# A state space block whose rows of B are spread from DRAM, with the first group's work divided differently

## The chip, the cores and the metric

The kernel runs on one core of a Trainium2 chip. Its time is the device time of one execution in microseconds (us); where several executions were timed, the median is given. The core's engines work side by side and each runs its own instructions in order: TensorE (PE in the profile, its weight loads PEld), VectorE (DVE), ScalarE (ACT), GpSimd (POOL), and SyncE (SP), which issues nearly all DMA transfers.

## The reference

The input is 16 sequences of 256 tokens with 128 features, in float32. Four blocks follow one another, each added to its input after a layer norm: a state space block, a local attention block with a feed-forward part (two layers), a power attention block, and the local attention block again. The change touches the first one, cut here to its core:

```python
x = resid * rsqrt(mean(resid**2) + 1e-5) * norm_w
skip, xe = x @ skip_w.T, x @ in_w.T
xs = silu(causal_conv4(xe) + conv_b)              # 256 channels
delta = softplus(xs @ wd1.T @ wd2.T + wd2_b)
A = -exp(A_log); Bm = xs @ wb.T; Cm = xs @ wc.T   # 16 states
h[t] = exp(delta[t] * A) * h[t-1] + (delta[t] * xs[t]) * Bm[t]
y[t] = sum over states of h[t] * Cm[t]
out = resid + ((y + xs * W_D) * silu(skip)) @ out_w.T
```

## The kernel before, in words

**Tiles.** The state space block (`ssm_block`) takes two sequences at a time as a group: 8 groups of 512 columns (C), the 256 channels as two halves of 128 partitions (e = 0 and 1). The 16 states of a group are 16 ticks, 128 ticks in all. A tick is: `spread` (a DMA that copies one row of B to all 128 partitions, tile bb, 256 KB, four buffers), `decay` (two ScalarE exponentials into PSUM, tile a, two of them in turn), `inputs` (GpSimd, bx = dx * bb, 128x1024), `scan` (VectorE, hs), `rows_of_c` (TensorE spreads a row of C into PSUM, c_ps, one bank), `products` (hs * c on VectorE, or on GpSimd for ticks 0, 3 and 8) and `add` (TensorE adds to y_ps).

**A group's preparation.** `moments_of` (VectorE) and `factors` (GpSimd) give the norm's scales; `normed_rows` (ScalarE) writes four tiles of rows, xr; `turn` (TensorE) transposes them into xrT_ps and `turned` (ScalarE) reads that into xrT; `conv` multiplies by the four taps' weights cw, eight products of 512 columns for the two halves, into xe_ps; `conv_out` (ScalarE) reads it into xs. `rows` and `reps` multiply xs by the weights of delta and C, and of B. For B the weights are repeated eight times (wrep, lines 152 to 162), so that `reps` gives a 128-row tile in which row p is B's row p mod 16; `reps_out` copies it to SBUF, and `spread` reads its eight equal rows, each for 16 partitions (line 354). `steps_in`, `steps_out` and `logs` give the two terms of softplus, and `steps` (GpSimd) adds them, giving delta, and multiplies by xs, giving dx, for each half.

**Order.** Each engine's instructions are pinned to the order in which the program issues them (class `Pinned`). The first group's preparation is written out by hand (lines 427 to 510): the weights cw are made (the weights transposed into in_w_ps, multiplied by the taps on VectorE, transposed into cw_ps half by half, each half copied to SBUF by ScalarE), then normed rows, turn, convolution, and so on through `steps`, the first two decays, the casts `second` and `third`, the first two `inputs` (lines 503 and 504), and then the normed rows, the turn and half of the convolution of the second group. Everything after that follows a written list (`written`, line 521), one round per group: each word is a step with its tick and its lag in groups. In it the read of a group's convolution (`co0`) stands ahead of the decays of ticks 2 and on, a group's `ro` (reps_out) stands between the spreads of ticks 12 and 13 of the group before (`sp12`, `sp13`), and its own first spread (`sp0`) follows three ticks later. After scan 0 and each third scan, one step of `fill` is run: a load or a preparation for the later blocks' weights (line 557), among them the scales of q and k (qs), which GpSimd multiplies into the rotation tables (rope).

Of the kernel before, what the change touches and what calls it, by code (L numbers as in the profile page):

```python
# [12 lines left out]
F32 = mybir.dt.float32  # L13
# [7 lines left out]
P = 128  # L21
D = 128
L = 256
E = 256
NST = 16
# [20 lines left out]
def kernel(ctx: ExitStack, tc: tile.TileContext, io, out: bass.AP):  # L46
    nc = tc.nc
# [13 lines left out]
    ident = const.tile([P, P], F32, name="ident")  # L61
# [5 lines left out]
    ones = const.tile([P, L], F32, name="ones")  # L67
# [51 lines left out]
    def ssm_block(fill):  # L119
        es = ExitStack()  # L120
        w = es.enter_context(tc.tile_pool(name="ssm_w", bufs=1))
        prep = es.enter_context(tc.tile_pool(name="ssm_prep", bufs=1))
        work = es.enter_context(tc.tile_pool(name="ssm_work", bufs=4))
        ps_m = es.enter_context(tc.tile_pool(name="ssm_psm", bufs=1, space=PSUM))
        ps_a = es.enter_context(tc.tile_pool(name="ssm_psa", bufs=1, space=PSUM))
        ps_c = es.enter_context(tc.tile_pool(name="ssm_psc", bufs=1, space=PSUM))
# [7 lines left out]
        NE = E // P  # L134
# [11 lines left out]
        def quarters(t):  # L146
            return t.rearrange("p (j i n) -> p j i n", j=NQ, i=2)

        wall = w.tile([P, NE, P], F32, name="wall")

        NR = P // NST
        wrep = w.tile([P, NE, P], F32, name="wrep")
        for e in range(NE):
            part = slice(e * P, (e + 1) * P)
            nc.sync.dma_start(quarters(wall[:, e])[:, :, 0, :], io["wd1T"][part].rearrange("p (j n) -> p j n", j=NQ))
            nc.sync.dma_start(
                quarters(wall[:, e])[:, :, 1, :], io["wcT"][part].unsqueeze(1).to_broadcast([P, NQ, NST])
            )
            nc.sync.dma_start(
                wrep[:, e].rearrange("p (j n) -> p j n", j=NR),  # L160
                io["wbT"][part].unsqueeze(1).to_broadcast([P, NR, NST]),
            )
        wd2T = w.tile([P, E], F32, name="wd2T")
        nc.gpsimd.memset(wd2T, 0.0)
        for j in range(NQ):
# [8 lines left out]
        pe, dve, act, pool, sp = (Pinned(e) for e in (nc.tensor, nc.vector, nc.scalar, nc.gpsimd, nc.sync))  # L174
# [4 lines left out]
        C = GS * L  # L179
# [3 lines left out]
        def bank(shape, name):  # L183
            return ps_m.tile(shape, F32, name=name, tag="m")
# [4 lines left out]
        for i in range(2):  # L189
            t = ps_a.tile([P, NE, GS, L], F32, name=f"a{i}")  # L190
# [4 lines left out]
        for i in range(2):  # L195
            t = w.tile([P, GS, PAD + L], F32, name=f"xrT{i}")
# [3 lines left out]
        groups = [{} for _ in range(NG)]  # L200
# [27 lines left out]
        def scaled(q, h, a, tag):  # L228
            t = prep.tile([P, GT, D], F32, name=f"{tag}_{h}", tag=tag)
            for i in range(GT):  # L230
                act.activation(
                    t[:, i, :], x4(h)[:, i, :], AF.Identity, bias=q["m"][:, a, i : i + 1],
                    scale=q["f"][:, a, i : i + 1],
                )
            return t

        def normed_rows(h, q):
            q["xr"] = scaled(q, h, 1, "xr")

        def turn(h, q):  # L240
            q["pt"] = bank([P, GS, L], f"xrT_ps_{h}")
            xr = q.pop("xr")
            for i in range(GT):
                pe.transpose(q["pt"].rearrange("p s t -> p (s t)")[:, i * P : (i + 1) * P], xr[:, i, :], ident)

        def turned(h, q):
            act.activation(xrTs[h % 2][:, :, PAD:], q.pop("pt"), AF.Copy, scale=norm_w)
            q["xs"] = prep.tile([P, NE, C], F32, name=f"xs_{h}", tag="xs", bufs=2)
# [33 lines left out]

        def reps(h, q, at=None):

            q["pb"] = bank([P, C], f"reps_ps_{h}") if at is None else at
            for e in range(NE):
                pe.matmul(q["pb"], wrep[:, e, :], q["xs"][:, e, :], start=(e == 0), stop=(e == NE - 1))

        def reps_out(h, q):
            q["reps"] = prep.tile([P, C], F32, name=f"reps_{h}", tag="reps", bufs=2)  # L290
            act.copy(q["reps"], q.pop("pb"))

        def rows(h, q):
            q["pr"] = bank([P, C], f"rows_ps_{h}")
# [5 lines left out]
        def rows_out(h, q):  # L300
            q["rows"] = prep.tile([P, C], F32, name=f"rows_{h}", tag="rows")
            act.copy(q["rows"], q["pr"])
            q["cb"] = prep.tile([P, C], BF16, name=f"cb_{h}", tag="cb", bufs=2)
            act.copy(q["cb"], q["pr"])
# [12 lines left out]
        def third(h, q):  # L317
            p = slice(2 * QW, 3 * QW)
            act.copy(q["cb"][p], q.pop("pr")[p])
# [16 lines left out]
            act.activation(av, av, AF.Exp, scale=-1.0)  # L336
            act.activation(av, av, AF.Ln, bias=1.0)

        def steps(h, q, e):
            if e == 0:  # L340
                q["dx"] = prep.tile([P, NE, C], F32, name=f"dx_{h}", tag="dx", bufs=2)
            delta = q["delta"][:, e, :]
            pool.tensor_add(delta, delta, q["av"][:, e, :])
            pool.tensor_mul(q["dx"][:, e, :], delta, q["xs"][:, e, :])


        TICKS = NG * NST
# [3 lines left out]
        def spread(i):  # L351

            bb = live["bb", i] = work.tile([P, C], F32, name=f"bb_{i}", tag="bb")
            src = groups[i // NST]["reps"][i % NST :: NST, :].unsqueeze(1).to_broadcast([NR, NST, C])
            sp.dma_start(bb, src)

        def decay(i):
# [5 lines left out]
                    AF.Exp, scale=neg_a[:, e, n : n + 1],  # L363
                )

        def inputs(i):
            bx = live["bx", i] = work.tile([P, NE, C], F32, name=f"bx_{i}", tag="bx")
            bb = live.pop(("bb", i)).unsqueeze(1).to_broadcast([P, NE, C])
            pool.tensor_mul(bx, groups[i // NST]["dx"], bb)

        def scan(i):
            hs = live["hs", i] = work.tile([P, NE, C], F32, name=f"hs_{i}", tag="hs")
# [68 lines left out]
        factors(0, groups[0])  # L441
        py = ps_y.tile([P, NE, C], F32, name="cw_ps", tag="y")
        pts = [py[:, e].rearrange("p (k m) -> p k m", k=DCONV) for e in range(NE)]
        for e in range(NE):
            dve.tensor_tensor(
                tap[:, e], pi[:, e].unsqueeze(1).to_broadcast([P, DCONV, P]),
                conv_w[:, e].unsqueeze(2).to_broadcast([P, DCONV, P]), ALU.mult,
            )
            for k in range(DCONV):
                pe.transpose(pts[e][:, k, :], tap[:, e, k, :], ident)  # L450
            act.copy(cw[:, :, e * P : (e + 1) * P], pts[e])

        sel = w.tile([3 * QW, NST, P], BF16, name="sel")
        wdd = w.tile([P, NE, P], F32, name="wdd")
# [2 lines left out]
        def more_weights():  # L457
            pool.memset(sel, 0.0)
            for j in range(3):
                part = sel[j * QW : (j + 1) * QW]  # L460
                pool.affine_select(
                    out=part, in_=part, pattern=[[-1, NST], [0, P]], compare_op=ALU.not_equal,
                    fill=1.0, base=-NST, channel_multiplier=1,
                )
            pool.tensor_scalar(nidentb, identb, -1.0, None, ALU.mult)
            for e in range(NE):
                pool.tensor_scalar(wdd[:, e, :], ident, w_d[:, e : e + 1], None, ALU.mult)


        q, r = groups[0], groups[1]  # L470
        normed_rows(0, q)
        turn(0, q)
        turned(0, q)
        more_weights()
        py = ps_y.tile([P, NE, C], F32, name="xe_ps_0", tag="y")
# [6 lines left out]
        factors(1, r)  # L482
        rows(0, q)
        rows_out(0, q)
        pb = ps_c.tile([P, C], F32, name="reps_ps_0", tag="c")
        reps(0, q, pb)
        pv = ps_y.tile([P, NE, C], F32, name="d2_ps_0", tag="y")
        for e in range(NE):
# [5 lines left out]
        for e in range(NE):  # L494
            steps_out(0, q, e)
            logs(0, q, e)
            steps(0, q, e)
        for i in range(2):
            decay(i)
        second(0, q)  # L500
        less_second(0, q)
        third(0, q)
        for i in range(2):
            inputs(i)
        rows_of_c(0)
        normed_rows(1, r)
        turn(1, r)
# [27 lines left out]
        for word in written.split():  # L535
            name, step, more, lag = re.fullmatch(r"((l1|l2|s2|s3|[a-z]+)[0-9.]*):(\d+)", word).group(1, 2, 1, 3)
# [5 lines left out]
        for i in range(NG + max(lag for _, _, lag, _ in parts)):  # L542
            for step, more, lag, name in parts:
                h = i - lag
                if (name, h) in done or not (0 <= h < NG or (step is silus and h == NG)):
                    continue
                if step in by_state:
                    step(h * NST + more[0])
                elif step is silus and h == NG:
                    silus(NG, None)  # L550
                elif step is conv:
                    e, half = more
                    conv(h, groups[h], e, range(2 * half, 2 * half + 2))
                else:
                    step(h, groups[h], *more)

                if step is scan and fill is not None and more[0] % 3 == 0:
                    next(fill, None)
# [928 lines left out]
    es = ExitStack()  # L1487
    w = es.enter_context(tc.tile_pool(name="pw_w", bufs=1))
    rest = es.enter_context(tc.tile_pool(name="rest", bufs=1))
    dram = es.enter_context(tc.tile_pool(name="pw_d", bufs=3, space=bass.MemoryType.DRAM))  # L1490
# [10 lines left out]
    for block, length, ahead in (  # L1501
# [4 lines left out]
        start = end - ahead  # L1506
# [58 lines left out]
```

## Time and profile before

| what | value |
|---|---|
| median of 3 runs | 2170.4 us (2170.24 to 2171.72) |
| the profiled execution's own time | 2171.14 us |
| its span, first to last instruction | 2169.3 us |
| mean granted TensorE clock | 0.981 |
| state space block | 0 to 492 us |
| first scan on VectorE | 39.97 us |
| one group later on, 95.00 to 149.41 | 54.41 us: VectorE busy 52.99, GpSimd 51.94, TensorE 51.61, ScalarE 42.23 |
| spread of a row of B | 128 transfers of 256 KB, issued by SP in some 0.6 us each |

A row of the timeline gives the start in us, the time the instruction (or a run of xN alike) took, the engine, the operation, output <- inputs with their sizes, and in brackets the idle time of the engine before it with what the profile believes ended it. A row of the chain of waits gives a start, a length and what the end of the kernel was waiting for in that time; "issue" is time that no wait explains. In the busy time of a stretch the columns are the stretch, its length, the busy time of PE, PEld, DVE, ACT and POOL with the count of instructions, the granted clock of TensorE, the share of time in which the DMA engines were busy, and GB/s. Clock records and the completions of a DMA (its landing) are read from the same trace.

### The profile page before, as it was taken

The numbers are of one execution on the slowest core, as the hardware profiler recorded it, in microseconds if no ns is written. First come the engines' busy times: TensorE is split into PE (matmuls) and PEld (weight loads), VectorE is DVE, ScalarE is ACT, GpSimd is POOL, SyncE is SP. The second block draws the span as 40 slices with busy tenths as digits, with TensorE's granted clock in tenths as the row PEclk, the third lists the DMA queues.
The fourth block names the chain that finished last, engine by engine and source line by source line (L and its number), as shares of the span: only waits on it lengthen the run. The fifth ranks groups of instructions, "written<-read, shape, count | busy, mean of one in ns | idle before, by whom it ended". The sixth has DMA issues, their size and how long they took to land.

```text
span 2169.3 us, 44282 instructions
## 1 busy us (share of the span) xinstructions
PE 2028.6 (94%) x16172; PEld 1331.3 (61%) x16174; DVE 1841.5 (85%) x3285; ACT 1706.5 (79%) x2879; POOL 1899.4 (88%) x2183
## 2 busy tenths in 40 slices
PE   5999999877999999999998999998899999999997
PEld 2344444334667777777765777775567777777775
DVE  2999999997989888888856999997988888888873
ACT  4777777746888887887865999997788887878874
POOL 7999999967999888888967999996999988888993
PEclk8999999998999999999997999999999999999998
DMA  4333333321001110111103323230010111101110
GB/s 93 97 83 81 98 80 79 79 52 24 18 22 23 23 23 17 23 23 23 23 11 118 101 98 119 84 114 9 21 23 17 23 23 23 23 16 33 28 28 23
DMA packets 97350, 104.21 MB, mean 48 GB/s; under 512 B 51458, under 2 KB 63596, under 8 KB 97132
## 3 DMA queue, kind: packets, MB, share of 16 engines
q1 hardware_dynamic: 96444, 101.22, 18.4%
q8 instruction: 128, 2.10, 0.4%
q14 instruction: 90, 0.74, 0.1%
q10 hardware_dynamic: 688, 0.15, 0.1%
HBM read 40.28 MB, written 2.36 MB: 20 GB/s over the span
## 4 chain that ended last, share of the span: by engine, by line
PE 54%; POOL 17%; DVE 9%; ACT 9%; issue 7%; DMA 2%; SPq 2%; POOLq 0%; DVEq 0%; ACTq 0%
PE bank L88 44%; POOL bx L88 7%; PE pair L88 7%; POOL mem L88 7%; DVE mem L88 6%; ACT mem L88 5%; DVE hs L88 2%; ACT pair L88 2%; SPq L88 2%; POOL hs L88 1%; PE xe_ps L88 1%; DMA mem<-u_all 1%; DMA bb<-reps 1%; POOL sf L88 1%; PE y_ps L88 1%
## 5 line engine op out<-in xcount | busy, mean ns | idle before, releaser
L88 POOL TENSOR_TENSOR mem<-mem 128x256 f32<-128x256 f32 (+5 forms) x1328 | 1156.7, 901 | 88.4 <-DVE mem L88 66.2
L88 ACT COPY mem<-bank 128x512 f32<-128x512 f32 (+4 forms) x1152 | 590.7, 556 | 147.6 <-PE bank L88 142.0
L88 PEld LDWEIGHTS bank<-ident,mem 128*128 128x128 f32 x3104 | 353.5, 141 | 171.2 <-issue 109.4
L88 PE MATMUL bank<-ident,mem 128*128 128x128 f32 x3104 | 426.0, 277 | 15.1 <-POOL mem L88 10.2
L88 PE MATMUL bank<-wqkv,mem 128*128 128x512 f32 x768 | 385.8, 607 | 1.8 <-ACT mem L88 1.8
L88 DVE TENSOR_REDUCE mem<-mem 128x8 f32<-128x512 f32 (+1 forms) x384 | 325.6, 849 | 9.8 <-ACT mem L88 9.4
L88 DVE TENSOR_TENSOR mem<-bank,rope 128x1024 f32<-128x1024 f32 x256 | 308.8, 1216 | 24.1 <-POOL mem L88 15.8
L88 DVE TENSOR_TENSOR_SCAN hs<-a,bx 128x1024 f32<-128x1024 f32 x128 | 291.4, 2281 | 38.6 <-POOL bx L88 35.5
L88 POOL TENSOR_TENSOR bx<-dx,bb 128x1024 f32<-128x1024 f32 x128 | 298.5, 2357 | 4.0 <-DVE hs L88 3.3
L88 ACT ACTIVATE mem<-mem 128x1024 f32<-128x1024 f32 (+2 forms) x384 | 280.2, 735 | 24.4 <-DVE mem L88 16.3
L88 PE MATMUL pair<-mem 64*64 64x128 f32 (+2 forms) x4096 | 256.7, 296 | 22.0 <-DVE mem L88 13.5
L88 PE MATMUL y_ps<-hs,ident 128*128 128x512 f32 x512 | 242.8, 599 | 11.4 <-DVE hs L88 6.7
L88 PEld LDWEIGHTS pair<-mem 64*64 64x64 f32 (+2 forms) x4096 | 194.9, 160 | 74.2 <-issue 26.2
L88 ACT ACTIVATE a<-delta,neg_a 128x510 f32<-128x510 f32 x256 | 176.0, 689 | 79.1 <-DVE hs L88 73.5
L88 ACT ACTIVATE mem<-bank 128x512 f32<-128x512 f32 (+1 forms) x272 | 160.6, 591 | 62.9 <-PE bank L88 58.6
L88 PE MATMUL bank<-mem 128*64 128x64 f32 (+2 forms) x4608 | 203.3, 255 | 5.3 <-ACT mem L88 2.9
L88 PE MATMUL bank<-mem,w 128*128 128x512 f32 x384 | 193.5, 603 | 3.8 <-ACT mem L88 3.8
L88 PEld LDWEIGHTS bank<-mem 128*64 128x64 f32 (+1 forms) x4608 | 156.8, 128 | 64.3 <-issue 30.1
L88 PEld LDWEIGHTS y_ps<-hs,ident 128*128 128x128 f32 x512 | 95.7, 190 | 154.4 <-issue 125.8
L88 DVE TENSOR_REDUCE mem<-pair 128x8 f32<-128x1024 f32 x128 | 153.2, 1197 | 30.3 <-PE pair L88 29.6
L88 PEld LDWEIGHTS bank<-wqkv,mem 128*128 128x128 f32 x768 | 128.9, 194 | 72.4 <-issue 60.2
L88 DVE TENSOR_TENSOR mem<-pair,mem 128x1024 f32<-128x1024 f32 x128 | 155.5, 1215 | 0.4
(130 smaller groups left out, 2827.0 us busy)
## 6 DMA issues: line engine op xcount, KB each, us to landing
bb<-reps SPq DMA_DIRECT2D x128, 256.0 KB
mem<-pngd SPq DMA_DIRECT2D x64, 512.0 KB
mem<-mem SPq DMA_DIRECT2D x128, 128.0 KB
mem<-u_all SPq DMA_DIRECT2D x64, 64.0 KB
mem<-u_all SPq DMA_DIRECT2D x64, 63.5 KB
x_all<-in_resid_dram SPq DMA_DIRECT2D x8, 256.0 KB
out_dram<-x_all SPq DMA_DIRECT2D x8, 256.0 KB
wqkv<-in_wqkv_dram SPq DMA_DIRECT2D x6, 256.0 KB
```

The source lines that it names most:

```text
L88: bi = getattr(self.eng, name)(*args, **kw)
```

## The change

Four edits, all in the state space block:

1. B's rows go by way of DRAM. The repeated weights wrep become wb with 16 columns; `reps` gives 16 rows; `reps_out` copies them to SBUF and issues a DMA of 32 KB to a DRAM tile; `spread` reads one row of that tile for all 128 partitions.
2. For the first group `steps` and the `inputs` of ticks 0 and 1 run on VectorE. The first `inputs` comes ahead of the decays in the program, the second right after scan 0.
3. The first group's normed rows are issued ahead of ScalarE's copy of the second half of cw, where they stood behind it.
4. Five extra products (`warm`), the identity times a tile of ones of 256 columns, into a bank that nothing reads: two ahead of cw's transposes, one behind each half of them, one behind the first group's turn.

```diff
+        dram = es.enter_context(tc.tile_pool(name="ssm_d", bufs=2, space=bass.MemoryType.DRAM))
...
-        wrep = w.tile([P, NE, P], F32, name="wrep")
+        wb = w.tile([P, NE, NST], F32, name="wb")
...
-            nc.sync.dma_start(
-                wrep[:, e].rearrange("p (j n) -> p j n", j=NR),
-                io["wbT"][part].unsqueeze(1).to_broadcast([P, NR, NST]),
-            )
+            nc.sync.dma_start(wb[:, e], io["wbT"][part])
...
-                pe.matmul(q["pb"], wrep[:, e, :], q["xs"][:, e, :], start=(e == 0), stop=(e == NE - 1))
+                pe.matmul(q["pb"], wb[:, e, :], q["xs"][:, e, :], start=(e == 0), stop=(e == NE - 1))
...
-            q["reps"] = prep.tile([P, C], F32, name=f"reps_{h}", tag="reps", bufs=2)
-            act.copy(q["reps"], q.pop("pb"))
+            t = prep.tile([NST, C], F32, name=f"reps_{h}", tag="reps", bufs=2)
+            act.copy(t, q.pop("pb"))
+            q["reps"] = dram.tile([NST, C], F32, name=f"repsd_{h}", tag="repsd")
+            sp.dma_start(q["reps"], t)
...
-        def steps(h, q, e):
+        def steps(h, q, e, eng=pool):
...
-            pool.tensor_add(delta, delta, q["av"][:, e, :])
-            pool.tensor_mul(q["dx"][:, e, :], delta, q["xs"][:, e, :])
+            eng.tensor_add(delta, delta, q["av"][:, e, :])
+            eng.tensor_mul(q["dx"][:, e, :], delta, q["xs"][:, e, :])
...
-            src = groups[i // NST]["reps"][i % NST :: NST, :].unsqueeze(1).to_broadcast([NR, NST, C])
+            src = groups[i // NST]["reps"][i % NST : i % NST + 1, :].to_broadcast([P, C])
...
-        def inputs(i):
+        def inputs(i, eng=pool):
...
+        warm_bank = ps_c.tile([P, C], F32, name="warm_ps", tag="c")
+
+        def warm(times):
+
+            for _ in range(times):
+                pe.matmul(warm_bank[:, :L], ident, ones, start=True, stop=True)
+
+        warm(2)
         for e in range(NE):
...
                 pe.transpose(pts[e][:, k, :], tap[:, e, k, :], ident)
+            if e == 1:
+                normed_rows(0, groups[0])
             act.copy(cw[:, :, e * P : (e + 1) * P], pts[e])
+            warm(1)
...
-        normed_rows(0, q)
         turn(0, q)
+        warm(1)
         turned(0, q)
...
-            steps(0, q, e)
+            steps(0, q, e, dve)
+        inputs(0, dve)
         for i in range(2):
             decay(i)
...
-        for i in range(2):
-            inputs(i)
...
+                if step is scan and (h, *more) == (0, 0):
+                    inputs(1, dve)
```

More of the change, by code (lines that the diff above doesn't have):

```diff
@@ L149, in ssm_block @@
         wall = w.tile([P, NE, P], F32, name="wall")
-        NR = P // NST
-        wrep = w.tile([P, NE, P], F32, name="wrep")
+        wb = w.tile([P, NE, NST], F32, name="wb")
         for e in range(NE):
@@ L283, in reps @@
         def reps(h, q, at=None):
-            q["pb"] = bank([P, C], f"reps_ps_{h}") if at is None else at
+            q["pb"] = bank([NST, C], f"reps_ps_{h}") if at is None else at
             for e in range(NE):
-                pe.matmul(q["pb"], wrep[:, e, :], q["xs"][:, e, :], start=(e == 0), stop=(e == NE - 1))
+                pe.matmul(q["pb"], wb[:, e, :], q["xs"][:, e, :], start=(e == 0), stop=(e == NE - 1))
         def reps_out(h, q):
-            q["reps"] = prep.tile([P, C], F32, name=f"reps_{h}", tag="reps", bufs=2)
-            act.copy(q["reps"], q.pop("pb"))
+            t = prep.tile([NST, C], F32, name=f"reps_{h}", tag="reps", bufs=2)
+            act.copy(t, q.pop("pb"))
+            q["reps"] = dram.tile([NST, C], F32, name=f"repsd_{h}", tag="repsd")
+            sp.dma_start(q["reps"], t)
         def rows(h, q):
@@ L364, in decay @@
                 )
-        def inputs(i):
+        def inputs(i, eng=pool):
             bx = live["bx", i] = work.tile([P, NE, C], F32, name=f"bx_{i}", tag="bx")
             bb = live.pop(("bb", i)).unsqueeze(1).to_broadcast([P, NE, C])
-            pool.tensor_mul(bx, groups[i // NST]["dx"], bb)
+            eng.tensor_mul(bx, groups[i // NST]["dx"], bb)
         def scan(i):
@@ L484, in ssm_block @@
         rows_out(0, q)
-        pb = ps_c.tile([P, C], F32, name="reps_ps_0", tag="c")
+        pb = ps_c.tile([NST, C], F32, name="reps_ps_0", tag="c")
         reps(0, q, pb)
```

## The prediction

> **What bounds the kernel now.** The diff touches the first of four stages, the state space block (0 to 492 us), so I read the chain of waits from the start, then the timeline of each engine, then busy time by stretch. From 62 us on the block is VectorE's. The busy time of one group of two sequences, and of the next (columns after the stretch: its length, then busy time of PE, PEld, DVE, ACT, POOL):
>
> ```profile
> 95.00:149.41 54.41, 51.61 (x142) 23.09 (x141) 52.99 (x39) 42.23 (x67) 51.94 (x32) 1.00 0.39 90
> 149.41:203.69 54.28, 51.48 (x141) 22.87 (x140) 52.48 (x39) 42.09 (x67) 51.81 (x30) 1.00 0.36 80
> ```
>
> VectorE works 53.0 of 54.4 us, GpSimd 51.9. Nothing in the diff takes work from VectorE there. The chain does name a transfer of a B row once a group, but it is an innocent link:
>
> ```profile
> 95.00 4.36 DMA bb<-reps
> 99.94 4.50 POOL bx L88 x2
> ```
>
> The row lands at 99.36, and GpSimd, busy with earlier products until 99.9, takes it at 99.94: 0.58 us to spare. So what the change can win lies ahead of 62 us, and there the chain of waits is:
>
> ```profile
> 10.47 0.50 ACT xr L88
> 10.97 0.04 issue
> 11.02 1.64 PE xrT_ps L88 x4
> 12.66 0.02 issue
> 12.69 0.70 ACT xrT L88
> 13.38 0.14 issue
> 13.52 5.80 PE xe_ps L88 x8
> ...
> 20.09 3.72 PE xe_ps L88 x8
> ...
> 34.96 1.23 POOL delta L88
> 36.19 0.02 issue
> 36.21 1.30 ACT a L88 x2
> ...
> 43.65 6.11 PE xe_ps L88 x8
> ```
>
> The same eight convolution products take 5.80 us at 13.52 and 3.72 at 20.09: the first are at half rate. Weight loads of that stretch come every 0.86 us up to 17.06 and every 0.43 from 17.86; the clock records change at 17.79. After ScalarE's decays (36.21) the chain goes on through the casts, the second group's normed rows and its convolution (43.65) to 62 us. VectorE waits for that chain:
>
> ```profile
> 39.97 4.60 DVE L88 TENSOR_TENSOR_SCAN hs<-a,bx 128x1024 f32<-128x1024 f32 x2 [26.36 <-POOL bx L88]
> 52.36 2.29 DVE L88 TENSOR_TENSOR_SCAN hs<-a,bx 128x1024 f32<-128x1024 f32 x1 [7.79 <-POOL bx L88]
> ```
>
> The second row's releaser is misleading: the third bx was done at 44.56. What ended at 52.26 was ScalarE's decay for scan 2, which stands in ScalarE's order behind the read of the second group's convolution (49.78). So the first two scans have 7.8 us of slack behind them.
>
> **Part by part.**
>
> *Normed rows sooner.* Their factors are ready on GpSimd at 9.54 (9.31 + 0.23), while ScalarE is free from 8.79. Today the second copy of cw stands ahead of them, so the first row starts at 10.47. After: 9.54 + 0.04 = 9.58, and the four end at 11.23 (1.65). The copy of cw now comes behind them and ends at about 11.75, when the turn's products are done too (before, 0.53 behind the last row: 11.76). xrT starts at about 11.8 and the convolution at 12.6: **-0.9**.
>
> *Extra products.* Each moves 256 columns of the same type as the convolution's 512, so half its rows: 0.43 us at half rate, 0.21 at full. Two run at 4.6 to 5.4, where PE idles until 7.04; one at 8.2 to 8.6, where it waits for the copy of cw until 8.84; one at 10.0 to 10.4, ahead of a turn whose last row comes at 11.23; one while ScalarE reads the turn. In each place PE idles longer than they last, so they cost nothing; without that cover 5 x 0.43 = 2.1. What they may buy is the clock. The clock records stand on a grid of 3.413 us (17.79, 34.86, 48.51 are 0, 5 and 9 steps). PE was busy 2.48 of 3.41 us in the step ending at 14.37 and the clock stayed low; in the next one it was busy throughout and got full rate at its end. Elsewhere steps of 0.94 to 1.00 full-width work raised it, those of 0.77 and less did not. Now PE works 7.04 to 8.60, 8.84 to 11.76 and 11.8 to 12.2: about 0.9 of the step 7.55 to 10.96, so full rate from 10.96. The convolution then takes 3.72 as at 20.09: **-2.08**. [...]
>
> *Sums and products on VectorE.* Only the second half's sum is on the chain. ScalarE's logarithm of it ends at 34.60; GpSimd, held by the first half's product, sums from 34.91 to 36.17, and the decay starts at 36.21. No row shows VectorE on two SBUF tensors. Ends: nothing (0.0) and GpSimd's 1.27. The nearest row is VectorE's own 128x512 product (tap, 0.69), which I take: sum done at 34.66 + 0.69 = 35.35, decay at 35.39: **-0.82** (-1.2, bound by the first decay's end at about 35.0, to -0.25). The other five moved instructions (0.69 x 3, two bx at 1.20 like the products from PSUM) run while VectorE idles, 26.4 us ahead of scan 0 and 7.8 behind scan 1; bx 1, queued ahead of scan 1, delays it, not scan 2. If that cover were gone: 4.5 us. What is late next is the second group's convolution, unchanged at half rate, since PE still idles some 8.6 us ahead of it (two whole steps); its 6.11 may be 5.4 to 6.9 with the grid's place.
>
> [...]
>
> *B's rows by DRAM.* The weight loads become 8 KB instead of 64; nothing waits for them. The product has 16 output rows, but moves 512 columns as before (0.43 each); the copy (0.58) likewise. Added: a 32 KB write per group, and SP's wait for it. Nearest rows: the power block's 16 KB writes, issue 0.32, landing 1.4 to 3.25 us. In group 0 behind SP's wait stand spreads 0 to 2: copy done at 25.7, written by 27.2 to 29.0, spread 0 landed 3 to 4.4 later (the 256 KB loads of x_all and wqkv take 3.1 to 4.7), at 30 to 33.4, which is when dx is ready (about 33); late by even 5 us it would hide in the 7.8. In later groups the copy ends 2.5 to 6.6 us ahead of the next spread in SP's order (68.65 against 71.17 in group 1), and the group's own first spread comes 17 us later. For the spreads: today, but for the first four, they land 4.25 to 5.8 us after issue and count 9 completions; DRAM sources such as the power block's 512 KB count 16 and land in 3.9 alone, 4.8 to 8.0 in fours. For 256 KB I expect about 3. Since rows are not awaited, gain 0; one place excepted. At 213.79 GpSimd waits 0.48 for q's and k's scales, queued behind a spread (issued 208.70, landed 213.10); with faster spreads that goes: **-0.4**, passed on because PE and VectorE wait for GpSimd's next product there.
>
> **Sum**: -0.9 - 2.08 - 0.82 - 0.4 = -4.2. The profiled execution took 2171.14 (span 2169.3 and 1.84 around it), 0.74 above the median 2170.4 of the runs shown, within the 1.5 us by which they differ. From its own time: 2166.9; from the median, which I predict: **2166.2**.
>
> **Rivals.**
> (a) The clock does not come early. For: the extra products leave gaps of 0.24 and some 0.4 us, and where the grid falls is seen only once; if no step is full enough until the convolution itself, it stays 5.8. Against: the shares above. 2166.2 + 2.1 = 2168.3.
> (b) More is won at 219 us. There PE idles 2.22 us for GpSimd's late product, its step is 1.38 of 3.41 busy, and the clock falls:
>
> ```profile
> 219.17:222.58 3.41, 1.38 (x4) 0.31 (x2) 3.41 (x3) 2.65 (x4) 3.41 (x2) 1.00 0.49 115
> 222.59:226.00 3.41, 3.23 (x4) 1.33 (x5) 0.57 (x1) 3.38 (x4) 3.41 (x3) 0.50 0.41 115
> ```
>
> Four products then take 3.58 in place of 1.9. With GpSimd 0.4 earlier the step is over half busy; one of 0.54 at 482 us kept the clock. 2166.2 - 1.7 = 2164.5. Against: the other runs may not have had that fall.
> (c) Slower: rows from DRAM land late. Every spread reads one 2 KB row 128 times. GpSimd has 0.58 us at the tightest link and 2.5 idle a group; so from a landing of 4.36 + 0.58 + 2.5 = 7.4 us on, VectorE starves. At 9.0, the worst of today's spreads (when four were queued), 1.6 a group x 7 = 11: 2177. Against: DRAM rows above.
> [...]
>
> **Chances.** Main case with (d) 0.50, itself 2165.0 to 2167.4; (a) 0.25; (b) 0.20; (c) 0.05. The range takes in (b) with the second group's convolution at its best (0.7 less, 2163.8) and (a) with it at its worst (0.8 more, 2169.1). About 0.2% (4.3 us, to 2166.06) is what a measurement can tell from no change. The main case straddles it: 0.25 of its 0.50 below, (b) nearly all, (a) hardly: faster 0.45, same 0.50, slower 0.05.
>
> **What would show it.** First xr at 9.6; convolution from 12.6 lasting 3.7 (right) or 5 and more (a); decay of the second half within 1 us of the logarithm's end; scan 2 some 3.8 us sooner, at 48.5, after a wait of over 5 us, whatever bx does; groups still 54.3 us; spreads landing in 3 to 4 us with 16 completions; no wait for the scales. Wrong if the groups change length by over 1 us, or scan 2 waits for bx or bb.

## The result, and the profile after

The changed kernel takes **2167.37 us**, median of 19 runs (2165.54 to 2170.02), beside 2170.87 for the kernel before, median of 19 (2169.22 to 2175.66): ratio 0.9983, 95% interval 0.9976 to 0.9990, or 3.5 us less. That is within 0.2%, the likeliest of the three outcomes. The forecast was 2166.2 in a range of 2163.8 to 2169.1. The profiled execution after took 2165.88 us (span 2164.0, mean granted clock 0.982), before 2171.14. Two executions far outside all others, the profiled one of e6 (5119.97 us) and one of e7 (2594.53 us), are not part of any ratio below.

The chain of waits after, in the stretch that was shown for before (start, length, what the end waited for):

```profile
8.91 0.94 PE cw_ps L88 x4
9.85 0.85 PE warm_ps L88 x2
10.70 0.85 PE xrT_ps L88 x4
11.56 0.75 PE warm_ps L88 x2
12.43 3.69 PE xe_ps L88 x8
...
31.08 0.64 ACT av L88
31.74 0.70 DVE delta L88
32.53 1.31 ACT a L88 x2
...
39.99 6.79 PE xe_ps L88 x8
```

Three things are to be seen. The first convolution lasts 3.69 us, not 5.80: the clock records show full rate from 12.08. The sum (DVE delta) takes 0.70 and the decay follows the logarithm's end (31.71) by 0.82, where it was 1.61. And the second group's convolution (39.99) starts 3.66 us sooner but lasts 6.79 where it took 6.11: full rate comes only at 46.21. Before's chain had no extra products in it; here TensorE goes from cw through the turn to the convolution with two of them on the way and hardly a gap, and the first takes 0.85 us as **two** instructions ("x2").

VectorE's second and third scan (in brackets the idle time ahead and what the profile puts it down to):

```profile
38.03 2.29 DVE L88 TENSOR_TENSOR_SCAN hs<-a,bx 128x1024 f32<-128x1024 f32 x1
49.38 2.29 DVE L88 TENSOR_TENSOR_SCAN hs<-a,bx 128x1024 f32<-128x1024 f32 x1 [9.06 <-ACT a L88]
```

Scan 0 starts 5.5 us sooner (34.52), scan 1 4.3, but scan 2 only 2.98: it waits 9.06 us for ScalarE's decay, behind the second group's convolution. From there the lead stays 2.9 to 3.0 up to scan 40, since the groups are as long as before (busy time by stretch; length, then PE, PEld, DVE, ACT, POOL):

```profile
92.00:146.40 54.40, 51.64 (x142) 22.53 (x140) 52.94 (x39) 42.31 (x67) 51.91 (x32) 1.00 0.30 91
146.40:200.70 54.30, 51.72 (x142) 22.53 (x141) 52.86 (x39) 42.32 (x67) 51.81 (x30) 1.00 0.27 81
```

The lead is 3.28 at scan 44, 3.93 at scan 52 and 3.69 at the block's last scan (477.49 against 481.18). The other 1.5 us of the profiled difference of 5.2 arise in the later blocks, which the change does not touch. From the last scan to the end, the thirteen profiles of this study that show the clock take 1685.1 to 1689.8 us, whatever the kernel. So an execution's total is good to a few us, and stage times are what the experiments below are read by.

### The profile page after: what moved, and what is told of

Its sections match the earlier page's. It is cut to its first block, busy times and chain, and to the rows that moved or that the text cites. A ratio compares the mean times of both kernels' runs of the same rounds, so it can differ in the third digit from the quotient of the medians.

```text
span 2164.0 us, 44300 instructions
## 1 busy us (share of the span) xinstructions
PE 2027.4 (94%) x16184; PEld 1327.1 (61%) x16184; DVE 1846.0 (85%) x3291; ACT 1709.8 (79%) x2879; POOL 1892.6 (87%) x2177
## 3 DMA queue, kind: packets, MB, share of 16 engines
HBM read 73.72 MB, written 2.62 MB: 35 GB/s over the span
## 4 chain that ended last, share of the span: by engine, by line
PE 55%; POOL 17%; DVE 9%; ACT 9%; issue 7%; SPq 1%; DMA 1%; POOLq 0%; DVEq 0%; ACTq 0%
PE bank L88 44%; POOL mem L88 7%; PE pair L88 7%; POOL bx L88 7%; DVE mem L88 6%; ACT mem L88 4%; DVE hs L88 2%; ACT pair L88 2%; SPq L88 1%; POOL hs L88 1%; ACT a L88 1%; DMA mem<-u_all 1%; PE xe_ps L88 1%; PE y_ps L88 1%; POOL sf L88 1%
```

## The experiments

Times are medians beside runs of the kernel before on the same chip. Parts alone come first, then the clock, then the rows of B.

**e1: the extra products alone**, on the kernel before.

```diff
+        warm(2)
...
             act.copy(cw[:, :, e * P : (e + 1) * P], pts[e])
+            warm(1)
...
         turn(0, q)
+        warm(1)
```

> The kernel before with the five extra products alone. Theory (the extra products lift TensorE's clock a step early): the first convolution still starts at about 13.5 us but takes about 3.7 in place of 5.8 us, everything behind it 1.5 to 2.1 earlier; median about 2169 against 2170.9. Rival (the first convolution was slow for another reason, such as the weight loads that the change made smaller): it stays at 5 to 6.9 us and the kernel at 2170.9.

Measured: 2169.47 against 2171.32, ratio 0.9990 (0.9981 to 1.0000). TensorE's timeline of it:

```profile
11.07 1.63 PE L88 MATMUL xrT_ps<-ident,xr 128*128 128x128 f32 x4 [0.21 <-ACT xr L88]
12.49 1.06 PE L88 MATMUL warm_ps<-ones,ident 128*128 128x256 f32 x2
13.57 5.16 PE L88 MATMUL xe_ps<-xrT,cw 128*128 128x512 f32 x8
```

The convolution still takes 5.16 us; full rate came at 16.58. The turn waits for rows that come late, one by one, and takes 1.63 in place of 1.06. The step of the grid from 9.76 to 13.17 was 0.94 busy by the records and did not lift the clock.

**e2: the change without the extra products.** The five calls of `warm` are taken out.

> The changed kernel without the extra products. Theory: the convolution starts at 12.4 to 12.5 us as in the changed kernel (normed rows sooner is worth 1 us by itself) but takes 5.2 to 6.9, so scan 2 comes about 2 us later than in the changed kernel; median about 2169.3 against 2167.4. Rival: the convolution takes 3.7 here too and the time stays at 2167.4.

Measured: 2169.00, ratio 0.9987 (0.9978 to 0.9996). The convolution starts as early as in the changed kernel and runs at half rate:

```profile
12.55 6.08 PE L88 MATMUL xe_ps<-xrT,cw 128*128 128x512 f32 x8 [0.87 <-ACT xrT L88]
```

Full rate at 17.40. Neither edit alone has a short first convolution, in one profile each. Without both together it lasted 5.15 to 6.72 in six profiles (before, e1, e2, e3, e4, e9); with both, 3.67 in six (the changed kernel, e5, e7, e8, e11, e12) and 3.89 in the seventh (e10), each at another place of the grid. The rows sooner give the turn its rows in time, the products fill what is left.

**e3: sums and products on VectorE alone**, on the kernel before.

```diff
-            steps(0, q, e)
+            steps(0, q, e, dve)
+        inputs(0, dve)
...
+                if step is scan and (h, *more) == (0, 0):
+                    inputs(1, dve)
```

> The kernel before with the first group's sums and products on VectorE alone. Theory (only the second half's sum is on the chain): the sum takes 0.69 us as in the changed kernel, the second half's decay starts 0.8 us earlier, at 35.4; scan 0 comes about 4 us earlier but scan 2 only 0.8; median about 2170.1. Rival (VectorE waited for GpSimd's bx, as the releaser of its 7.8 us wait says): scan 2 comes 4 to 5 us earlier and the kernel is at 2166 to 2167.

Measured: 2169.57, ratio 0.9998 (0.9989 to 1.0007), which can't be told from no change. In the trace the decay follows the logarithm by 0.82 us, as in the changed kernel, and scan 2 follows it by 17.04 in place of 17.76: 0.7 us. The second product, on VectorE:

```profile
38.67 2.54 DVE L88 TENSOR_TENSOR bx<-dx,bb 128x1024 f32<-128x1024 f32 x1
```

It takes 2.54 in place of 1.23 (the first one's), beside a GpSimd product at 37.77 to 40.06. Scan 2 waits 7.09 us all the same, for ScalarE.

**e4: B's rows by DRAM alone**, on the kernel before (edit 1 of the diff, and nothing else).

> The kernel before with B's rows by way of DRAM alone. Theory: spreads land in about 3.2 us with 16 completions in place of 4.6 with 9; scan 4 stays where it was (61.8), groups stay at 54.3 to 54.4 us; the 0.48 us wait for the scales of q and k at 214 goes, so 0.4 less from there; median about 2170.5. Rival (the spreads of a group are on the path, as the chain of waits has it): each group 1 us shorter, 2164 or so; or, if the landing of the 32 KB write holds up SP, scan 4 later than 61.8 and the kernel slower.

Measured: 2170.34, ratio 0.9996 (0.9988 to 1.0005). The spreads land in 3.17 us (median; 16 completions) in place of 4.61 (9), the wait for the scales is gone, a group is 54.32. Scan 4 comes 1.6 us later than before (63.41 against 61.81), which was to be the sign of a spread held up by the write. It is not one: the first convolution took 6.72 us and the second group's 6.42 (before 5.79 and 6.10), 0.3 us went to the products into 16 rows, and no transfer stands in the chain of waits between 5 and 63 us. So apart from those 0.3 us nothing is lost by the way through DRAM, and nothing that a median can show is won.

**e5: the first two inputs back on GpSimd**, the sums still on VectorE.

```diff
-        inputs(0, dve)
...
+        for i in range(2):
+            inputs(i)
```

> The changed kernel with the first two inputs back on GpSimd behind the casts, the sums still on VectorE. Theory (only the second half's sum of the VectorE share is on the chain): bx 0 and 1 take 2.36 us on GpSimd, scan 0 comes some 1.2 us later, scan 2 stays where it is up to the clock's half-rate time (49 us); first convolution again 3.7 to 4.3 because its extra products leave no gap from 6.9 to 12.3; median within 0.7 of the changed kernel's 2167.4. Rival (the inputs bring part of the gain): scan 2 and the median 1 us or more later.

Measured: 2167.80 against 2171.29, ratio 0.9981 (0.9972 to 0.9990). Scan 0 comes at 35.77 in place of 34.52, scan 2 at 49.20 in place of 49.38. The two moved products buy nothing: what they win ends in the wait ahead of scan 2.

**e11: the extra products half as wide**, 128 columns.

```diff
-                pe.matmul(warm_bank[:, :L], ident, ones, start=True, stop=True)
+                pe.matmul(warm_bank[:, :P], ident, ones[:, :P], start=True, stop=True)
```

> The changed kernel with the five extra products of 128 columns in place of 256, so that each (two TensorE instructions) takes some 0.43 us at half rate, the duration that the prediction had given to the 256 columns. Theory that TensorE must be busy without gaps for the clock to rise: gaps of 0.4 to 0.8 us open again, full rate comes a step later in some places of the grid; the first convolution lasts 5 us or more, scan 2 comes 1 to 2 us later than in the changed kernel (49.4), 2168.5. Rival, that nine tenths of a step are enough as the prediction had it: convolution 3.7 us, scan 2 at 49 to 49.5, 2167.4.

Measured: 2164.97 against 2170.75, ratio 0.9977 (0.9968 to 0.9987). The rival was right, and the theory of no gaps falls:

```profile
12.46 3.67 PE L88 MATMUL xe_ps<-xrT,cw 128*128 128x512 f32 x8 [0.65 <-ACT xrT L88]
```

The step from 8.02 to 11.43 was 0.93 busy, with gaps of 0.25 us and the like, and lifted the clock. Since e1's 0.94 did not, 0.93 to 0.94 is not sure; but the short products are enough here.

**e7 and e8: keeping the clock for the second group's convolution.** e7 adds 18 products between the first group's last products and its scans; e8 adds four more in the three gaps ahead of the second group's convolution.

```diff
         reps_out(0, q)
+        for _ in range(18):
+            pe.matmul(keep_bank[:, :L], ident, ones, start=True, stop=True)
...
         less_second(0, q)
+        late(1)
         third(0, q)
...
+        late(2)
         turn(1, r)
+        late(1)
         turned(1, r)
```

> The changed kernel with 18 more extra products behind the first group's, which fill TensorE's idle time of 8.7 us ahead of the second group's turn (26.9 to about 34.7). Theory (the second group's convolution is on the chain and at half rate because TensorE idled two grid steps): if the pieces of work from 35.8 to 39.9 keep the clock, that convolution takes 3.7 in place of 5.8 to 6.9 us, scan 2 comes 2.1 to 3.1 us sooner and the median is about 2164.9; if those pieces are too thin a step, the clock falls again ahead of it and the gain is between 0 and 1. Rival (something other than the clock, such as VectorE or GpSimd, sets scan 2): no gain at full rate either.

> As the one with 18 more extra products, and four more in the gaps between the casts, ahead of the turn's products and behind them. Theory: the clock is at full rate through the second group's turn and convolution whatever the grid's place; convolution 3.7 us, scan 2 at about 46.5, all that follows 2.1 to 3.1 earlier than in the changed kernel; median about 2164.8. Rival: the products ahead of the turn hold it up by as much as they win, or scan 2 waits for something else: no gain.

Measured: e7 2168.47, ratio 0.9987 (0.9978 to 0.9996); e8 **2164.95** (2161.21 to 2166.6), ratio **0.9970** (0.9958 to 0.9981). In e7 the clock held to 38.58 and fell just ahead of the convolution, after a step (35.17 to 38.58) that was 0.52 busy:

```profile
39.81 6.47 PE L88 MATMUL xe_ps<-xrT,cw 128*128 128x512 f32 x8 [0.78 <-ACT xrT L88]
```

In e8 it never fell between 10.35 and 443.84:

```profile
36.67 1.03 PE L88 MATMUL late_ps<-ones,ident 128*128 128x256 f32 x4
37.54 0.93 PE L88 MATMUL xrT_ps<-ident,xr 128*128 128x128 f32 x4
38.30 0.60 PE L88 MATMUL late_ps<-ones,ident 128*128 128x256 f32 x2
39.24 3.70 PE L88 MATMUL xe_ps<-xrT,cw 128*128 128x512 f32 x8 [0.34 <-ACT xrT L88]
```

In e7 scan 2 comes at 48.89, half a microsecond ahead of the changed kernel's. In e8 it comes at 45.56 in place of 49.38 and the block's last scan at 474.15 in place of 477.49, so e8 beats both kernels in this stage, by 7.0 and 3.3 us. In the medians its lead over the kernel before is clear of noise; over the changed kernel it is not, as the two intervals just overlap (0.9958 to 0.9981 and 0.9976 to 0.9990).

**e6 and e12: the same DRAM row as 8 x 16 repeats.** Both runs have the same edit, and stages are read from e12.

```diff
-            src = groups[i // NST]["reps"][i % NST : i % NST + 1, :].to_broadcast([P, C])
+            src = groups[i // NST]["reps"][i % NST : i % NST + 1, :].unsqueeze(1).to_broadcast([8, 16, C])
```

> [...]

> The changed kernel with the same DRAM row handed to the DMA as 8 x 16 repeats. If the count of descriptors' outer steps sets how many engines share the transfer, then 9 completions and a landing of 4.3 to 5 us as in the kernel before, SP's issue back at 0.6 us, GpSimd waiting 0.4 us for the scales again, scans of the first group as in the changed kernel and groups of 54.3. If the source in DRAM sets it, 16 completions and 3.2 us.

Measured: e6 2166.23, ratio 0.9977 (0.9967 to 0.9986); e12 2166.37, one run. The completions are 9 again, SP's issue takes 0.58 us in place of 0.32, and the median landing is 3.86. So of the 1.43 us that a landing became shorter, the source (one row in DRAM for eight in SBUF) accounts for 0.75 (4.61 to 3.86, with 9 completions both times) and the form of the copy, with 16 completions in place of 9, for 0.68 (3.86 to 3.18); no run has 16 completions with the source in SBUF. How many DMA engines share a spread, no trace here shows: it counts completions. One thing was not as expected: GpSimd did not wait for the scales, although the rows landed later. SP had issued them 0.65 us behind a spread, as before, and GpSimd came to them at 209.18, 0.14 after they landed (205.73 + 3.31). The time is that of the changed kernel: the faster landing itself buys nothing.

**e9 and e10: three buffers for the rows in place of four**, in the kernel before and in the changed one. It takes cover away from the landing.

```diff
-            bb = live["bb", i] = work.tile([P, C], F32, name=f"bb_{i}", tag="bb")
+            bb = live["bb", i] = work.tile([P, C], F32, name=f"bb_{i}", tag="bb", bufs=3)
```

> The kernel before with three buffers for B's spread rows in place of four: a spread then waits for the product of one tick later. Worked out from the rows of before (each spread's own landing, issued at the end of the product three ticks earlier), eight rows land 0.3 to 1.35 us after the time at which GpSimd took them with four buffers: ticks 3, 24, 40, 72, 88, 104, 120 and 127, so one in nearly every group. Theory that the rows' landing is far from the bound even then: GpSimd idles some 2.5 us a group, takes the 0.4 to 1.1 us from that, and the groups stay 54.3 to 54.4; time 2171 within 1 us. Rival, that every late row passes to VectorE at once: groups 54.7 to 55.5, time 2174 to 2178.

> The changed kernel with three buffers for B's spread rows. By the same working from the rows of after no row lands late: the tightest is tick 19, 0.82 us ahead of its product. So groups of 54.3 and 2167.4 within 1 us. If it loses as much as the kernel before with three buffers, then landing time isn't what three buffers cost.

Measured: e9 2180.51 against 2170.75, ratio 1.0043 (1.0028 to 1.0058); e10 2174.56, ratio 1.0015 (1.0006 to 1.0024). Both are slower than expected, and hardly for the rows: no wait of GpSimd in the block is put down to one. From scan 16 to 32 and on to 48, e9 takes 54.52 and 55.19 us, 0.2 and 0.5 longer than before. The rest of the loss stands in two places, of which this is the first, on GpSimd, in the kernel before and in e9:

```profile
213.79 0.45 POOL L88 TENSOR_TENSOR rope<-rope_c,qs 128x128 f32<-128x128 f32 x1 [0.48 <-DMA qs<-in_k_scale_dram]
...
217.90 0.46 POOL L88 TENSOR_TENSOR rope<-rope_c,qs 128x128 f32<-128x128 f32 x1 [4.36 <-DMA qs<-in_k_scale_dram]
```

and this SP's order in e9:

```profile
203.93 5.61 SPq L88 DMA_DIRECT2D bb<-reps  x2
209.59 0.46 SPq L88 DMA_DIRECT2D b<-in_b_dram  x1
210.11 1.25 SPq L88 DMA_DIRECT2D lg<-in_ln_g_dram  x1
211.40 0.83 SPq L88 DMA_DIRECT2D lb<-in_ln_b_dram  x1
212.34 0.61 SPq L88 DMA_DIRECT2D bb<-reps  x1
212.99 0.46 SPq L88 DMA_DIRECT2D qs<-in_q_scale_dram  x1
```

A spread that waited for a buffer one tick longer held up the loads behind it in SP's queue: the first of the scales' loads was issued at 209.35 with four buffers and at 212.99 with three. GpSimd waits 4.36 us here (0.48 with four buffers) and 5.27 at 384.64 (0): 9.2 us more, of the 10.5 that the block is longer from scan 2 to its last scan. In e10 the same waits are 1.84 and 4.6 (6.5 in sum, none in the changed kernel), of 7.1 us by the same measure. Theory and rival both looked at the wrong product: what the landing and buffers of B's rows set here is when SP comes to the loads behind them.

## Why the prediction was right, step by step

**Normed rows sooner** (predicted -0.9): the first row at 9.28, the convolution 1.09 sooner. The working had the rows wait for the last factor on GpSimd (9.54); they wait only for sm (9.25). Part of the rest is that x_all landed 0.1 sooner.

**Extra products, the clock** (-2.08): 3.69 for 5.80, -2.12. The mechanism and the saving were right, the cost was mis-sized: each extra product is two instructions in the trace ("x2"), 0.85 us at half rate and not 0.43. (The eight rows that the working read as the eight products are four, of one half of the channels, and the second eight those of the other half.) That they still cost hardly anything (first row to convolution 3.15 us with them, 3.04 without, in e2) is luck of the place: they reach 12.31, ScalarE's read of the turn 12.29. The step "PE idles longer than they last" failed for the product behind the second half of cw: it ran 9.85 to 10.70 and the turn came after it, back to back. e11 shows that the size I had taken would have served as well. The working had full rate from 10.96, on the grid of the profile before. In the profile after the grid lay 1.1 us later: the step from 8.66 to 12.08 was busy throughout, and full rate came 0.35 us ahead of the convolution. Rival (a) did not occur with both edits, in seven profiles of seven; e1 and e2 are what it looks like.

**Sum on VectorE** (-0.82): -0.79. The nearest row (0.69 for VectorE's product of that size) was the right choice between the ends.

**No cost for the products into 16 rows** (0): this term was wrong by 0.3 us. The stretch from the second convolution to the logarithm's end is 0.32 longer than before. TensorE's timeline, before and after:

```profile
26.19 1.88 PE L88 MATMUL reps_ps<-xs,wrep 128*128 128x512 f32 x4
27.91 1.88 PE L88 MATMUL d_ps<-rows,wd2T 128*128 128x512 f32 x4
...
23.08 1.89 PE L88 MATMUL reps_ps<-xs,wb 128*16 128x512 f32 x4
24.90 1.98 PE L88 MATMUL d_ps<-rows,wd2T 128*128 128x512 f32 x4
```

The first of the four starts 1.06 us after the products ahead of it (0.96 before), d_ps 1.82 after that (1.72), and d_ps takes 1.98 (1.88): 0.1 us three times. e4 and e2 show the same three numbers, e1, e3 and e9 those of before, so it goes with the 16-column weights. Why, no run here shows.

**The second group's convolution** ("5.4 to 6.9 with the grid's place"): 6.79, +0.7, near the worst end. The step in which it began (39.38 to 42.80) was 0.82 busy and did not lift the clock. With the 0.3 above, this is what the forecast promised too much: -1.09 - 2.12 + 0.32 - 0.79 + 0.68 = -3.0 at scan 2, against -3.8 predicted (52.36 to 48.5).

**The scales** (-0.4): the wait of 0.48 is gone, and between scans 48 and 52 the lead grows by 0.64, of which 0.34 is given back by scan 56. Another 0.38 is won between scans 40 and 44, where a wait of 0.48 ahead of VectorE's product at 193.73 is gone. Those four ticks take 14.28 to 14.31 us in all nine profiles of kernels with the sum on VectorE, and 14.64 to 15.22 in the four without (before, e1, e4, e9). So it goes with the VectorE share of the first group; by what way, stays open.

**Rival (b)**: the clock fell at 220.29 as before, after a step 1.33 of 3.40 busy:

```profile
216.88:220.28 3.40, 1.33 (x3) 0.49 (x3) 3.00 (x2) 3.34 (x5) 3.40 (x3) 1.00 0.52 165
```

Its price was right and its condition wrong. In e1, e4 and e8 the clock did not fall there. Between scans 48 and 52 e1 gains 1.6 us with the scales' wait in it as before, e4 2.1 without that wait. The thin step was 0.48 to 0.50 busy in these three and 0.39 in the changed kernel, 0.40 before: how the gap lies on the grid decides, not GpSimd's 0.4 us alone.

**Rival (c)**: nothing landed late, but its threshold rested on a misread link. The transfer at 95.00 in the chain of before is not the row of the product at 99.94: counted tick by tick, that product is tick 17's and the row tick 19's. The chain puts a wait for several things down to one of them, and here it took the wrong one. The least time from a row's landing to its own product, from tick 3 on, is 2.51 us before (median 7.09), not 0.58, and 3.18 after (8.42). With the 2.5 us that GpSimd idles, the 7.4 us of the text should have been 4.37 + 2.51 + 2.5 = 9.4. e9, where the least of that cover is 0.13 us and the median 2.98, lengthened a group by 0.2 to 0.5 us.

**Rival (d)**, a VectorE share that buys nothing, did not occur: the sum took 0.70, where GpSimd's took 1.23, and the decay's -0.79 came of it.

## What to carry to other kernels

Read a stage's gain where its last wait ends: here 5.5 us at the first scan became 3.0 at the third, because the third waits for another chain, through the second group's convolution at half clock. e8, which kept the clock for that convolution as well, won 3.8 us more there, 3.1 of it in the convolution. Filler products paid here where they made a whole step of the grid busy (55 of 55 steps over 0.95 lifted the clock), or kept one from falling under six tenths (1812 of 1812 such steps held it); 18 of them with a thin step behind them (e7) bought half a microsecond. Before a transfer's landing is called tight, pair each transfer with its own consumer by number, and look at what stands behind its issue in the queue: that, and not the landing, was what lost most of the 9.8 us in e9.

## What the runs showed of the hardware

**The clock rose and fell at different shares of work.** In thirteen profiles, for each grid step of 3.413 us that begins in the first 560 us, the share in which TensorE was busy by the records, and whether the next step was at full rate:

| busy share of a step at half rate | full rate next | busy share of a step at full rate | full rate next |
|---|---|---|---|
| under 0.75 | 0 of 62 | under 0.40 | 0 of 35 |
| 0.75 to 0.80 | 0 of 15 | 0.40 to 0.50 | 9 of 39 |
| 0.80 to 0.85 | 3 of 5 | 0.50 to 0.60 | 82 of 86 |
| 0.85 to 0.95 | 24 of 25 | 0.60 and more | 1812 of 1812 |
| over 0.95 | 55 of 55 | | |

The one miss above 0.85 is e1. Later, in the changed kernel, the steps from 1158.95 and from 1169.19 us were busy throughout and did not lift the clock, which rose at 1176.02; 24 of the 52 products from 1162 to 1176 use only 32 of the 128 rows, and whether that is why, no run here shows. Up to 560 us, 55 of 55 steps over 0.95 lifted it. The grid's place differs from profile to profile: its first step begins anywhere from 0.00 to 3.37 us behind the first instruction.

**In two pairs of products VectorE and GpSimd held each other up.** GpSimd's first product after, with VectorE's of two SBUF inputs (1.22 us) beside it:

```profile
33.24 3.38 POOL L88 TENSOR_TENSOR bx<-dx,bb 128x1024 f32<-128x1024 f32 x1 [10.93 <-DVE dx L88]
```

It takes 3.38 in place of 2.36, nearly VectorE's length more, and VectorE's had begun first, at 33.19. In e3 GpSimd's began first (37.77 against 38.67), and it was VectorE that waited (2.54 for 1.23). In both pairs the product that began second was the longer one; by what way, no run here shows.

**128 reads of one 2 KB row** in DRAM by each spread, with 128 spreads, cost no engine anything that shows: the traffic from DRAM rose from 40.28 to 73.72 MB and the groups stayed 54.3 us.
